# A four-layer graph network on one core: the head and the first period given as one list of 403 steps

## The chip, the cores and the metric

The kernel runs on one core of a Trainium2 chip. A core has five engines that run side by side, each with its own queue of instructions in a fixed order: TensorE (PE, matmuls, with weight loads shown as PEld), VectorE (DVE), ScalarE (ACT), GpSimd (POOL) and SyncE (SP, which here only starts transfers). An instruction starts when the one ahead of it on its engine has gone and the semaphores it waits for have come. The metric is the device time of one execution in microseconds; the time before is the median of three runs.

## The reference

The input x has 128 graphs of 128 nodes with 256 features, adj is one 128x128 matrix for all of them. Four layers follow, each on h = relu(layernorm(x)) and each added to x:

```python
h = jnp.maximum(_layernorm(x, axis=-1), 0.0)
x = x + _L0_gnn_ref(h, adj, adj, ...)   # relu of three messages, each times a sigmoid gate of h
h = jnp.maximum(_layernorm(x, axis=-1), 0.0)
x = x + _L1_gnn_ref(h, adj, Wqkv, Wo)   # causal attention with adj as a bias
h = jnp.maximum(_layernorm(x, axis=-1), 0.0)
x = x + _L2_gnn_ref(h, adj, adj, W1, W2, W3)   # three products with adj*adj mixing the nodes
h = jnp.maximum(_layernorm(x, axis=-1), 0.0)
x = x + _L3_gnn_ref(h, adj, W1, b1, g1, be1, W2, b2, g2, be2)   # two linear layers with batchnorm
```

The batchnorms of the last layer take statistics over all graphs, so a second pass follows the first.

## The kernel before

The 128 graphs go in 32 groups of four. `layer0`, `layer1` (attention and the first product of layer 2), `layer2` and `layer3` are Python generators that emit the instructions of one group and yield at the ends of stages; a yield of `SPLIT` marks a place within a stage. `norm` takes the layernorm statistics on DVE (L367, L371), the power -0.5 on POOL (L224 for half a group, L375 to L378 for a whole one) and gives h on ACT (L392). `turn` (L405) transposes h on PE and evicts it with ACT and DVE; `mixed` (L435) multiplies by an adjacency matrix; `seven` (L498) multiplies two 2x2 block matrices with seven block products instead of eight, for which block sums of both operands are needed: `sums` (L447) makes those of the activations, `seven_of` (L234) those of the weights, both on DVE.

Main loop: in period g (L1000) the list `TURN` interleaves the streams A (layer 0 of group g+2), B and b (layer 1 of group g+1 and the start of g+2), C (layer 2 of g) and D and d (layer 3 of g-1 and the start of g). `in_turn` (L88) ties each new instruction to the one before it on its engine, so that the scheduler, which otherwise chooses the order on an engine, keeps the written one. For g of 1 and more this is done for all five engines (`PINNED`, L957), and period 0 is left to the scheduler.

Ahead of the loop stands the head (L982 to L999): group 0 is taken through layers 0 and 1 in two halves of two graphs (streams a and c for layer 0, b and d for layer 1), beside layer 0 of group 1 (A) and the preparation of the weights (p, `prepare`, L278). The string `FILL` gives the order in whole stages, of which only PE's order is kept (`KEPT`). Group 0 uses plain products instead of `seven`, since the block sums of w1, m_qk and w_vo are made only afterwards. The letter w calls `awake(12)`, which puts twelve transposes of the identity on PE (L110); their result is not read.

Preparation in `prepare`: the transposes of Wqkv (wqkvT, L259) and the products m_qk and w_vo (pqk, pvo, L289), then the mask and the square of adj, then the block sums of w2, m_qk, w_vo, w1 and w3, the transposes and sums of the last layer's weights (bw1T, bw2T), the degree normalisation of adj, and the vectors. Ahead of all this stand the transpose of adj (pa) and of the gate weights (pgw) and the two signed adjacency matrices ain and aout. The loads are queued on SP in the order x of group 0 (two halves), gate biases, Wqkv, Wo, edge biases, x of group 1, W1, W2, x of group 2, W3, gate weights, the last layer's weights and vectors; the three gate weight rows for pgw go by POOL's queue.

Of the kernel before, what the change touches and what calls it, by code (L numbers as in the profile page):

```python
# [8 lines left out]
FP = mybir.dt.float32  # L9
# [6 lines left out]
P = 128  # L16
# [6 lines left out]
def kernel(  # L23
# [209 lines left out]

    def seven_of(b, name, extra=None):  # L234


        b11, b21, b12, b22 = quarters(b)
        if extra is None:
            extra = weights.tile([P, 3, b.shape[1] // 2, b.shape[2] // 2], FP, name=f"{name}_s")
        operands = set_of(b, extra)  # L240
        t4n, t1, t2 = operands[3:6]
        nc.vector.tensor_tensor(t1, b12, b11, ALU.subtract)
        nc.vector.tensor_tensor(t2, b22, t1, ALU.subtract)
        nc.vector.tensor_tensor(t4n, b21, t2, ALU.subtract)
        nc.vector.tensor_tensor(b12, b22, b12, ALU.subtract)
        return operands

# [4 lines left out]
    def turned(dst, src, nr, name):  # L252


        ncol = src.shape[-1] // P
        for c in range(ncol):
            pt = bank([P, nr, P], f"{name}_{c}")
            for r in range(nr):
                nc.tensor.transpose(pt[:, r, :], src[:, r, c * P : (c + 1) * P], ident)  # L259
            nc.scalar.copy(dst[:, c, :].rearrange("p (r q) -> p r q", r=nr), pt)  # L260


    pa = bank([P, P], "pa")
    nc.tensor.transpose(pa, adj_sb, ident)
    nc.vector.tensor_copy(adjT, pa)
    pw = bank([P, DC, 3], "pgw")
    for c in range(DC):
        nc.tensor.transpose(pw[:, c, :], gwr[:, c * P : (c + 1) * P], ident[:3, :3])
    nc.vector.tensor_copy(gwT, pw)
    for dst, src in ((ain, adj_sb), (aout, adjT)):  # L270
        nc.vector.tensor_scalar(pos, src, 0.0, None, ALU.is_gt)
        nc.vector.scalar_tensor_tensor(f, src, 0.0, pos, ALU.min, ALU.add)
        nc.vector.tensor_tensor(dst, f, adj_sb, ALU.mult)

    SETS = {}
    plain = {"qv": 0, "u": 0}

    def prepare():  # L278


        turned(wT, wqkv, DC, "wqkvT")
        for dst, l0, right, name in (
            (m_qk, 0, wT[:, DC : 2 * DC, :], "pqk"),
            (w_vo, 2 * DC, wo, "pvo"),
        ):
            for i in range(DC):
                pw = bank([P, D], f"{name}_{i}")
                for j in range(DC):
                    nc.tensor.matmul(  # L289
                        pw, wT[:, l0 + j, i * P : (i + 1) * P], right[:, j, :],  # L290
                        start=(j == 0), stop=(j == DC - 1),
                    )
                nc.scalar.copy(dst[:, i, :], pw)
        yield

        nc.gpsimd.affine_select(
            out=maskb, in_=adj_sb, compare_op=ALU.is_ge, fill=NEG, base=0,
            pattern=[[-1, P]], channel_multiplier=1,
        )
        nc.vector.tensor_tensor(a2T, adjT, adjT, ALU.mult)  # L300
        yield
        SETS["2"] = seven_of(w2, "w2")
        yield

        assert plain == {"qv": 2, "u": 2}
        SETS["q"], SETS["v"] = seven_of(m_qk, "m_qk"), seven_of(w_vo, "w_vo")
        SETS["1"] = seven_of(w1, "w1")
        yield
        SETS["3"] = seven_of(w3, "w3")
        yield  # L310

        turned(bw1T, bw1, FC, "bw1T")
        turned(bw2t, bw2, DC, "bw2T")
        seven_of(bw2t, "bw2t", bw2s)
        nc.sync.dma_start(BW2S, bw2s)
        nc.sync.dma_start(BW2T, bw2t)
        yield

        nc.vector.tensor_tensor(an, adj_sb, ident, ALU.add)
        nc.vector.tensor_tensor(anT, adjT, ident, ALU.add)  # L320
        nc.vector.tensor_reduce(deg[:, 0:1], anT, AX.X, ALU.add)
        nc.vector.tensor_reduce(deg[:, 1:2], an, AX.X, ALU.add)
        nc.vector.scalar_tensor_tensor(
            dscr, an, 1.0, ident, ALU.mult, ALU.mult, accum_out=deg[:, 2:3]
        )
        nc.vector.tensor_tensor(deg[:, 3:4], deg[:, 0:1], deg[:, 1:2], ALU.add)
        nc.vector.tensor_tensor(deg[:, 3:4], deg[:, 3:4], deg[:, 2:3], ALU.subtract)
        inv_sqrt(dinv, deg[:, 3:4], 0.0)
        nc.vector.tensor_scalar(an, an, dinv, None, ALU.mult)
        ph = bank([P, P], "ph")  # L330
        nc.tensor.transpose(ph, an, ident)
        nc.vector.tensor_scalar(ahT, ph, dinv, None, ALU.mult)
        pv = bank([P, NV], "pv")
        nc.tensor.transpose(pv, vrow, ident[:NV, :NV])
        nc.vector.tensor_copy(vecs, pv)
        yield
        nc.scalar.copy(bw1T_12, bw1T[:, 0, F1 // 2 :])
        SETS["b"] = seven_of(bw1T, "bw1T")

# [65 lines left out]
    def turn(dst, h, bs, name):  # L405

        for c in range(DC):
            pt = bank([P, len(bs), P], f"{name}_{c}")
            for k, b in enumerate(bs):
                nc.tensor.transpose(pt[:, k, :], h[:, b, c * P : (c + 1) * P], ident)  # L410
            evict = nc.vector.tensor_copy if c else nc.scalar.copy
            evict(columns(dst, c, bs), pt.rearrange("p b n -> p (b n)"))

    Q = 32
# [20 lines left out]
    def mixed(dst, src, aT, name, evicts, bs=ALL):  # L435

        for c in range(src.shape[-1] // P):
# [7 lines left out]
            yield SPLIT  # L445

    def sums(engine, a, extra, s3=None):  # L447


        a11, a12, a21, a22 = a  # L450
        s3 = a21 if s3 is None else s3
        s1, s2, s4 = (extra[:, i] for i in range(3))
        engine.tensor_tensor(s1, a21, a22, ALU.add)
# [5 lines left out]
        engine.tensor_tensor(s3, a11, a21, ALU.subtract)  # L459
        return a11, a12, s4, a22, s1, s2, s3  # L460

# [78 lines left out]
    def layer0(g, bs=ALL):  # L540
# [9 lines left out]
        if g < 2:  # L550

            hT = tile_of(g, bs, [P, DC, T], "dT", f"h0T_{g}", 2)
            turn(hT, h, bs, f"ph_{tail}")
            yield
            pl = bank([P, n, 3], f"pl_{tail}")
            for k, b in enumerate(bs):
                for c in range(DC):
                    nc.tensor.matmul(
                        pl[:, k, :], hT[:, c, b * P : (b + 1) * P], gwT[:, c, :],
                        start=(c == 0), stop=(c == DC - 1),  # L560
                    )
            nc.vector.tensor_tensor(gl, pl, gate_bias, ALU.add)
        else:
# [56 lines left out]
        else:  # L620
            pc = bank([P, n, P], f"pc_{tail}")
            for k, b in enumerate(bs):
                nc.tensor.transpose(pc[:, k, :], cmb[:, b, :], ident)
            nc.vector.tensor_copy(cmbT[:, mine, :], pc)
        yield
# [16 lines left out]
    def layer1(g, bs=ALL):  # L642
# [14 lines left out]
        if swapped:  # L657
            cut(hT.rearrange("p c t -> p (c t)"), blocks, DC * G)
        else:
            turn(hT, h, bs, f"pt_{tail}")  # L660
        if n == G:
# [29 lines left out]
        else:  # L691
            for i in halves:
                for j in range(DC):
# [7 lines left out]
                    for rr in range(2):  # L701
                        at = (2 * i + rr) * P
                        for c in range(DC):
# [3 lines left out]
                                start=False, stop=(c == DC - 1), skip_group_check=True,  # L707
                            )
                    evict = nc.vector.tensor_copy if j else nc.scalar.copy
                    evict(qv[:, i, j], pb)  # L710
            plain["qv"] += 1
            yield
# [41 lines left out]
        else:  # L754
            pp = bank([P, n, P], f"pp_{tail}")
            for k in range(n):
                nc.tensor.transpose(pp[:, k, :], p[:, k, :], ident)
            nc.vector.tensor_copy(pT, pp)
        yield
# [41 lines left out]
        else:  # L801
            for b in bs:
                pb = bank([P, H1], f"pu_{g}_{b}")
                for c in range(DC):
                    nc.tensor.matmul(
                        pb, mT[:, c, b * P : (b + 1) * P], w1[:, c, :],
                        start=(c == 0), stop=(c == DC - 1),
                    )
                nc.scalar.activation(u[:, b, :], pb, AF.Relu)
            plain["u"] += 1  # L810
            yield
        uT = tile_of(g, bs, [P, HC1, T], "uT", f"uT_{g}", 1)
        yield from mixed(uT, u, a2T, f"pmu_{tail}", (nc.vector.tensor_copy,), bs)
        if bs[-1] == G - 1:
            ex = w.tile([P, 3, HC1 // 2, T // 2], FP, tag="us", name=f"us_{g}", bufs=1)
            US[g] = yield from sums(nc.vector, quarters_t(uT), ex)
        yield
# [159 lines left out]
    def part(f, g):  # L977
# [3 lines left out]

    KEPT = (mybir.EngineType.PE,)  # L982
    FILL = "aacaaccacapcabpccpbdbdAdbdAdddbAbbAdwbAbAAdpppbdp"
    HALVES = range(G // 2), range(G // 2, G)
    stream = {
        "a": layer0(0, HALVES[0]), "c": layer0(0, HALVES[1]), "p": prepare(),
        "b": layer1(0, HALVES[0]), "d": layer1(0, HALVES[1]), "A": part(layer0, 1),
    }
    for k in FILL:
        at = len(nc.cur_bb.bb.instructions)  # L990
        if k == "w":
            awake(12)
        else:
            step(stream[k])
        in_turn(at, KEPT)
    assert all(next(stream[k], k) == k for k in "acbdA")
    bs, ds = part(layer1, 1), stream["p"]
    for _ in range(BEGUN):
        next(bs)  # L999
    for g in range(NG):  # L1000
        if g + AHEAD < NG:
# [7 lines left out]
        for k in TURN if g < LAST else ():  # L1009
            at = len(nc.cur_bb.bb.instructions)  # L1010
            next(stream[k], None)
            if g:
                in_turn(at, PINNED)
        for k in FINAL if g == LAST else ():
# [247 lines left out]
```

## Time and profile before

| what | value |
|---|---|
| median of the runs | 2534.65 us (2533.94 to 2539.27) |
| profiled execution, its own time | 2536.71 us |
| profiled execution, span | 2534.7 us |
| PE, DVE, ACT, POOL busy in the span | 98%, 78%, 47%, 12% |
| PE matmuls | 14832 |
| first matmul of period 1 (p_1_0_x) | 139.67 us |
| first matmul of period 2 (p_2_0_x) | 208.69 us |

The span runs from the first to the last instruction of the profile. In a table by stretches each row has the stretch, its length, and for PE, PEld, DVE, ACT and POOL the busy time with the number of instructions in brackets; then the granted clock of PE (1.00 is full), the mean busy share of the DMA engines, and what they moved in GB/s. In a list by time each row has start, length, engine, line, operation, the tile written and the tiles read, and in square brackets the idle time of the engine ahead of it and what ended that.

### The profile page before, as it was taken

To read this page: it belongs to the slowest core of one execution; us is meant where nothing else is said; L and a number is where in the kernel's file an instruction comes from. 1 tells how busy PE (TensorE), PEld (TensorE's weight loads), DVE (VectorE), ACT (ScalarE), POOL (GpSimd) and SP (SyncE) were. 2 spreads that over 40 slices of the span, in tenths; PEclk is the share of its full clock that TensorE was granted. 3 is DMA by queue.
4 is the path that set the end of the run, shared out by engine and by line. 5 is a ranking of instruction groups with operands and counts; after the bars stand their busy time and mean duration, and the time that the engine had idled before them with its cause. 6 is when DMAs were issued, how large, how long until landed. Compare 5 with 4: busy or idle time off the path is not lost.

```text
span 2534.7 us, 40786 instructions
## 1 busy us (share of the span) xinstructions
PE 2483.4 (98%) x14832; PEld 2246.1 (89%) x14832; DVE 1970.5 (78%) x4861; ACT 1180.4 (47%) x2486; POOL 311.4 (12%) x563
## 2 busy tenths in 40 slices
PE   6999999999999999999999999999999999999996
PEld 5899999999999999999999999999999999888875
DVE  6777787777778877788777777887778777558876
ACT  3444444444444444444444444444444444337766
POOL 1111111111101111111111111111111111000001
PEclk9999999999999999999999999999999999999998
DMA  4112222222221122222222222122222112135559
GB/s 136 32 51 67 67 63 63 59 67 67 59 59 49 54 66 67 67 67 60 59 66 67 59 59 57 51 61 67 68 67 62 59 55 59 34 131 200 174 192 389
DMA packets 115180, 206.54 MB, mean 81 GB/s; under 512 B 11538, under 2 KB 77092, under 8 KB 111012
## 3 DMA queue, kind: packets, MB, share of 16 engines
q1 hardware_dynamic: 108404, 180.80, 23.4%
q0 software_dynamic: 6432, 23.07, 2.6%
q8 instruction: 117, 1.92, 0.3%
q14 instruction: 83, 0.68, 0.1%
q10 hardware_dynamic: 144, 0.07, 0.0%
HBM read 105.20 MB, written 98.70 MB: 80 GB/s over the span
## 4 chain that ended last, share of the span: by engine, by line
PE 94%; DMA 2%; DVE 2%; ACT 1%; POOL 0%; issue 0%; SPq 0%; DVEq 0%; POOLq 0%; ACTq 0%
PE p_x L490 17%; PE p_x L473 9%; PE p_z L490 9%; PE pmu L440 5%; PE p_z L473 4%; PE p_y L490 4%; PE po_x L1134 4%; PE pz_x L490 4%; PE pu_x L473 4%; PE p_y L473 2%; PE pg L440 2%; PE py L764 2%; PE ps L720 2%; PE pm L630 2%; PE pm L440 2%; PE pr L873 2%
## 5 line engine op out<-in xcount | busy, mean ns | idle before, releaser
L392 ACT ACTIVATE h<-x,sh,rs 128x256 f32<-128x256 f32 x512 | 266.7, 590 | 482.9 <-POOL sh L378 471.3
L490 PE MATMUL p_x<-uT,w 128*128 128x256 f32 x1024 | 242.1, 379 | 0.0
L844 ACT ACTIVATE h2T<-h2T 128x512 f32<-128x512 f32 x192 | 121.0, 630 | 256.7 <-DVE h2T L842 256.7
L490 PEld LDWEIGHTS p_x<-uT,w 128*128 128x128 f32 x1024 | 189.8, 190 | 23.2
L375 POOL TENSOR_SCALAR rs<-mv 128x4 f32<-128x4 f32 x124 | 37.2, 300 | 1378.8 <-DVE mv L371 1365.4
L367 DVE BATCH_NORM_STATS2 st<-x 128x6 f32<-128x256 f32 x512 | 185.9, 414 | 3.3
L567 DVE SCALAR_TENSOR_TENSOR gs<-h,gw 128x256 f32<-128x256 f32 x360 | 152.3, 423 | 43.0 <-ACT h L392 31.5
L440 PEld LDWEIGHTS pmu<-a2T,u 128*128 128x128 f32 x1024 | 124.2, 192 | 29.6 <-issue 21.8
L505 ACT COPY p_t<-p_x 128x512 f32<-128x512 f32 (+1 forms) x192 | 97.4, 507 | 76.2 <-PE p_x L473 69.8
L376 POOL TENSOR_TENSOR rs<-rs,nhalf 128x4 f32<-128x4 f32 x124 | 128.7, 1038 | 9.8
L473 PE MATMUL p_x<-w,h2T 128*128 128x128 f32 x1024 | 124.7, 275 | 0.0
L440 PE MATMUL pmu<-a2T,u 128*128 128x128 f32 x1024 | 124.5, 275 | 0.0
L473 PEld LDWEIGHTS p_x<-w,h2T 128*128 128x128 f32 x1024 | 121.9, 192 | 1.7
L490 PE MATMUL p_x<-us,w_s 128*128 128x256 f32 x512 | 121.1, 379 | 0.0
L490 PE MATMUL p_z<-us,w 128*128 128x256 f32 x512 | 121.1, 379 | 0.0
L490 PE MATMUL p_x<-uT,w_s 128*128 128x256 f32 x512 | 121.1, 379 | 0.0
L490 PE MATMUL p_z<-us,w_s 128*128 128x256 f32 x512 | 121.0, 379 | 0.0
L490 PE MATMUL p_y<-uT,w 128*128 128x256 f32 x512 | 120.9, 379 | 0.0
L842 DVE TENSOR_TENSOR h2T<-p_z,p_t 128x512 f32<-128x512 f32 x64 | 44.0, 687 | 89.4 <-PE p_z L490 89.4
L490 PEld LDWEIGHTS p_x<-uT,w_s 128*128 128x128 f32 x512 | 97.1, 190 | 13.4 <-DVE h2T L842 0.3
L490 PEld LDWEIGHTS p_z<-us,w_s 128*128 128x128 f32 x512 | 97.3, 190 | 13.2
L490 PEld LDWEIGHTS p_y<-uT,w 128*128 128x128 f32 x512 | 97.3, 190 | 13.2
(331 smaller groups left out, 5994.2 us busy)
## 6 DMA issues: line engine op xcount, KB each, us to landing
z<-zo SPq DMA_DIRECT2D x62, 512.0 KB, 5.1
zi<-z SPq DMA_DIRECT2D x31, 1024.0 KB, 4.9
x<-x POOLq DMA_DIRECT2D x32, 512.0 KB, 3.4
x<-in_x_dram SPq DMA_DIRECT2D x31, 512.0 KB, 3.9
hc<-h SPq DMA_DIRECT2D x120, 128.0 KB, 2.4
h<-hc SPq DMA_DIRECT2D x30, 512.0 KB, 4.2
out_dram<-x3i SPq DMA_DIRECT2D x30, 512.0 KB, 11.7
x3i<-x SPq DMA_DIRECT2D x20, 512.0 KB, 6.5
```

What stands on the lines that cost most here:

```text
L367: nc.vector.bn_stats(st[:, k, :], xt[:, b, :])
L376: nc.gpsimd.tensor_tensor(rs, rs, nhalf[:, :n], ALU.pow)
L392: nc.scalar.activation(dst, src, AF.Relu, bias=sh[:, k : k + 1], scale=rs[:, k : k + 1])
L440: nc.tensor.matmul(pm[:, k, :], src[:, b, c * P : (c + 1) * P], aT, start=True, stop=True)
L473: nc.tensor.matmul(pb[:, rr, :], a_r[r][:, c, rr * P : (rr + 1) * P], b_r[r][:, c, :wide], start=(first and rr == 0 and c == 0), stop=(c = ...
L490: nc.tensor.matmul(pb[:, jj, :], b_r[r][:, c, at : at + P], a_r[r][:, c, :], start=(first and jj == 0 and c == 0), stop=(c == nk - 1), ski ...
L505: nc.scalar.copy(t, pb)
L567: nc.vector.scalar_tensor_tensor(gs, h[:, b, :], 1.0, gw[:, i, :], ALU.mult, ALU.mult, accum_out=gl[:, k, i : i + 1],)
L630: nc.tensor.matmul(pm[:, r, :], cmbT[:, b, :], h[:, b, :], start=True, stop=True)
L720: nc.tensor.matmul(ps[:, k, :], qv[:, b // 2, c, 0, (b % 2) * P : (b % 2 + 1) * P], hT[:, c, b * P : (b + 1) * P], start=(c == 0), stop=(c ...
L844: nc.scalar.activation(dst, dst, AF.Relu)
L1134: nc.tensor.matmul(pb, BW2R[r][:, c, :], a_r[r][:, c, :], start=(first and c == 0), stop=(c == FC // 2 - 1), skip_group_check=True,)
```

## The change

- `prepare` is cut into five generators: `gate_weights` (i), `attention_weights` (p), `mixing_weights` (m), `network_weights` (n) and `last_weights` (o). They yield after each instruction or small group; `weight_sums` makes the block sums of one weight in four steps.
- The tiles for the block sums of all weights are allocated at once (`SETS`), ahead of the streams.
- `turn`, `layer0` and `layer1` get more `SPLIT` yields between PE's work and its eviction.
- `FILL`, `awake(12)` and the unpinned period 0 give way to `HEAD`, a string of 403 letters. Each letter takes one step of one stream up to its next yield of either kind, and `in_turn` keeps the order on all five engines. The streams are a, c, b, d as before, e and f (layers 0 and 1 of group 1), A (layer 0 of group 2), B (start of layer 1 of group 2), C (layer 2 of group 0), D (start of layer 3 of group 0), and the five chains of weights. The loop then starts at period 1 with the same `TURN`.

```diff
-    def seven_of(b, name, extra=None):
...
+    SETS = {}
+    for k, b in ("2", w2), ("1", w1), ("3", w3), ("q", m_qk), ("v", w_vo), ("b", bw1T):
+        _, nk, nf = b.shape
+        SETS[k] = set_of(b, weights.tile([P, 3, nk // 2, nf // 2], FP, name=f"set_{k}"))
+
+    def weight_sums(operands):
+
+        b11, b21, b22, t4n, t1, t2, b12 = operands
         nc.vector.tensor_tensor(t1, b12, b11, ALU.subtract)
+        yield
         nc.vector.tensor_tensor(t2, b22, t1, ALU.subtract)
+        yield
         nc.vector.tensor_tensor(t4n, b21, t2, ALU.subtract)
+        yield
         nc.vector.tensor_tensor(b12, b22, b12, ALU.subtract)
-        return operands
+        yield
...
-    def prepare():
-
-
-        turned(wT, wqkv, DC, "wqkvT")
+    def gate_weights():
...
+    def attention_weights():
+
+        yield from turned(wT, wqkv, DC, "wqkvT")
...
+        yield from weight_sums(SETS["q"])
+        yield from weight_sums(SETS["v"])
...
+    def network_weights():
+
+        yield from weight_sums(SETS["2"])
+        yield from weight_sums(SETS["1"])
+        yield from weight_sums(SETS["3"])
+
+    def last_weights():
+
+        yield from turned(bw1T, bw1, FC, "bw1T")
+        yield from turned(bw2t, bw2, DC, "bw2T")
+        yield from weight_sums(set_of(bw2t, bw2s))
+        nc.sync.dma_start(BW2S, bw2s)
+        nc.sync.dma_start(BW2T, bw2t)
+        yield
...
-    KEPT = (mybir.EngineType.PE,)
-    FILL = "aacaaccacapcabpccpbdbdAdbdAdddbAbbAdwbAbAAdpppbdp"
     HALVES = range(G // 2), range(G // 2, G)
+    HEAD = (
+        "iiiaaaapppppcciiipmaapaammapccccacaeeppppppccaccaaceeaacapppppccbbeeecpp"
+        "ecbbbbebdeedAembbbbbededdddbbbeeeodbbmbbeedddbeooommdbooooooobbbbpdddeme"
+        "dbbbeddbedfffoobbbbbbpppdopdbbbbbbbbdCfffffdddfAAffnCCfffffffffAddddfofp"
+        "ofoAddddndpAAfffddddddddfdffddCddfCCCCCCffnnACCCCfCoAACCAACCACCCCCCCCCCA"
+        "AnnnnnAfCCCCCCoffffffAffffCCCCCCACCACCCCfffnCfAAAAABBBffffffffnCConBfBff"
+        "ffoofCCCfCffffooCCfffCCCCCDDDfffffffffffffB"
+    )
+    load_x(AHEAD)
+    ds, bs = layer3(0), layer1(2)
...
-    for k in FILL:
+    for k in HEAD:
         at = len(nc.cur_bb.bb.instructions)
-        if k == "w":
-            awake(12)
-        else:
-            step(stream[k])
-        in_turn(at, KEPT)
...
+        next(stream[k], None)
+        in_turn(at, PINNED)
...
-    for g in range(NG):
+    for g in range(1, NG):
```

## The prediction

> **What bounds the kernel now.** First the page: TensorE (PE) is busy nearly the whole span, and its only thin slice is the first (each slice is 63.4 us).
>
> ```profile
> PE 2483.4 (98%) x14832; PEld 2246.1 (89%) x14832; DVE 1970.5 (78%) x4861; ACT 1180.4 (47%) x2486; POOL 311.4 (12%) x563
> ...
> PE   6999999999999999999999999999999999999996
> ```
>
> Second, the busy times by stretch. From 100 us on PE has no gap: one period of the main loop, 139.67 to 208.69, is 69.02 us of PE busy in 69.02 us. Ahead of 70 us PE is the engine that waits, and in 40 to 60 us its granted clock is 0.84 besides.
>
> ```profile
> 0.00:10.00 10.00, 2.19 (x8) 1.24 (x8) 5.94 (x31) 3.81 (x7) 4.64 (x15) 1.00 0.70 214
> 10.00:20.00 10.00, 6.80 (x25) 5.67 (x26) 5.49 (x22) 3.66 (x11) 0.00 (x0) 1.00 1.05 385
> 20.00:30.00 10.00, 7.91 (x36) 6.46 (x35) 8.58 (x17) 4.19 (x12) 1.62 (x1) 1.00 0.74 209
> 30.00:40.00 10.00, 5.11 (x32) 4.20 (x32) 8.07 (x28) 3.83 (x10) 4.50 (x5) 0.99 0.16 54
> 40.00:50.00 10.00, 8.62 (x50) 7.54 (x50) 4.09 (x11) 3.68 (x12) 0.00 (x0) 0.84 0.00 1
> 50.00:60.00 10.00, 8.80 (x49) 7.30 (x49) 6.80 (x30) 4.92 (x13) 1.39 (x2) 0.83 0.00 0
> ...
> 139.67:208.69 69.02, 69.02 (x424) 62.95 (x423) 54.74 (x138) 31.02 (x67) 9.03 (x18) 1.00 0.22 62
> ```
>
> Third, PE in order of time, for which wait ends last.
>
> ```profile
> 7.88 0.34 PE L268 MATMUL pgw<-ident,wide 3*128 3x3 f32 x2 [4.22 <-DMA wide<-in_L_gnn_loop_gate_dram]
> 8.19 1.40 PE L410 MATMUL ph<-ident,h 128*128 128x128 f32 x4
> ...
> 20.57 2.53 PE L259 MATMUL wqkvT<-ident,wide 128*128 128x128 f32 x12
> ...
> 40.03 2.07 PE L696 MATMUL pqv<-hT,m_qk 128*128 128x256 f32 x4 [4.43 <-ACT hT L412]
> 41.90 1.68 PE L704 MATMUL pqv<-w_vo,hT 128*128 128x128 f32 x8
> 43.42 1.03 PE L696 MATMUL pqv<-hT,m_qk 128*128 128x256 f32 x4
> ...
> 57.07 1.47 PE L110 MATMUL awake<-ident 128*128 128x128 f32 x12
> ```
>
> The 4.43 us stall is the largest after the start: ACT's copy of hT stood behind h of group 1 (38.63), which waited on POOL, which worked beside DVE's two-input weight sums:
>
> ```profile
> 27.58 1.62 POOL L224 TENSOR_TENSOR rs<-rs,nhalf 128x2 f32<-128x2 f32 x1 [18.18 <-DVE rs L222]
> 32.92 0.69 POOL L224 TENSOR_TENSOR rs<-rs,nhalf 128x2 f32<-128x2 f32 x1 [3.72 <-DVE rs L222]
> ...
> 37.08 1.52 POOL L378 TENSOR_TENSOR sh<-sh,rs 128x4 f32<-128x4 f32 x1
> ```
>
> **The measure: lag.** From period 1 on (first matmul p_1_0_x, 139.67 us) PE has the same work in both lists, without a gap before, so the change is worth what it moves that start. I price the work ahead of it at the full-clock pitch of the rows: 128x128 0.1115 us (pmu, 32 in 3.57), 128x256 0.216 (p_x, 8 in 1.73), 128x512 0.431, 128x3 0.115 (pl at 51.40, 16 in 1.85); a transpose is one row, a matmul two. Before: 86x0.1115 + 34x0.115 + 226x0.216 + 300x0.1115 + 20x0.431 + 0.12 = 104.5 us. Lag = 139.67 - 104.5 = 35.2: some 22 idle, the rest half-speed matmuls. The changed list has the same PE work less the 12 transposes of awake: 103.2 us.
>
> **Part by part.** *awake removed*: 12x0.1115 = 1.3 us. *Preparation in five chains, the list over all engines, SPLIT yields*: DVE, ACT, POOL and SP issue exactly the same instructions, only in another order; SP's load queue stands as it was (BW2S and BW2T swap, read only in the second pass). The swap of p through DRAM (pc) now goes whole ahead of that of the gates (cc); there are 19.1 us of PE work from ps to py where there were 13.8, so both stay hidden. So everything else is waits. I walked the new queues: each instruction starts at the later of its engine's last end and its inputs' end plus 0.06 us, with durations from the rows (DVE: 0.33 for 128x256, 0.60 for 128x512, 1.14 for 128x1024, 0.20 for 128x128, bn 0.34; ACT: h 0.50, copies 0.28 and 0.49; pow 0.70, POOL's four-op chain 1.8). PE is at half speed to 24.5 us and again for 3.5 us after group 1's gate (below). The stations:
>
> - *Start.* adj lands at 3.1, adjT and ain now stand ahead of the statistics on DVE (0.83 us), but the second half's no longer do: h of half one ends at 7.75, its transposes start at 7.8 (before 8.19, behind the loop gate's DMA).
> - *wqkv.* Three wqkvT transposes now stand in PE's queue ahead of ph_0_1, so PE waits for that DMA, which before was never waited for. Bounds: in 1-us windows 1.387 MB had moved by 8.0, and wqkv ends the first 1.376 MB; x of group 1 ends 2.43 MB, which had moved by 10.8, and landed at 4.69+7.3 = 12.0. So 8.0 to 9.2; I take 9.0. Each us later costs one.
> - *Layer 0, half one.* DVE's gl of half two waits for pl_2, with half one's gate products queued behind it, and pl_2 waits behind six wqkvT and pqk_0 at half speed. pc_0 at 20.9, 3.7 us later than before (17.18).
> - *Layer 0, half two.* pm_1 at 27.9 (27.48): even. But now group 1's transposes and gate pl_1 are next, 2.7 us of work which before came at 46.96 and 51.40.
> - *Attention.* Half one's first pqv at 32.4 (31.37), half two's at 40.0 (40.03), but bw1T, ps_0 and group 1's gate are behind us, and exp, pc, py follow with PE fed: idle from 32 to 48 is under 1 us in the walk.
> - *Network.* pu_0 at 50.9 (61.15). Work ahead of it is 28.75 us: lag 22.1, as against 61.15 - 28.2 = 32.9 before. From there the walk has no stall up to p_0_0_z at 75.4 (work 53.24, lag 22.1).
> - *Stalls added by hand.* (a) Group 1's h for layer 1: its POOL chain starts beside five two-input weight sums (bw2t, set_q, set_v; 1.6 us). The chain took 2.05 us at 70.78 and 4.0 at 34.63 beside such sums; the walk's 1.8 leaves 0.4 of slack, so the stall is 0 to 1.8; as the sums cover part of the chain, I take 1.0. (b) pm_1_0_0 now follows p_0_z directly, 8.8 us of work after py. Before, h was ready 9.7 us after py began (108.48 to 118.2) and DVE's list adds two oeb products (0.8); four blocks follow ACT's pace: 1.0 us. (c) Drift from pitch rounding, as before between 100 and 139.67: 0.4.
>
> Sum: lag 22.1 + 1.0 + 1.0 + 0.4 = 24.5; p_1_0_x at 103.2 + 24.5 = 127.7 instead of 139.7: **12.0 us saved**. On the profiled execution 2534.7 becomes 2522.7 of span (its own time, 2536.71, 2524.7). The runs' median is 2534.65, 2.06 us under that execution, and 2534.65 - 12.0 = **2522.7 us**.
>
> **Two rules against rows.** Rows first: wqkvT at 20.57 takes 0.21 us per transpose, twice the later 0.111, although PE had been at work off and on since 8.19; the clock record says 1.00 there, so for the start I trust the durations. After the 4.43 us gap it reads 0.50 in 40 to 42, and full speed is back at 43.42, 3.4 us later; in 53.4 to 57, after small gaps and the gate's 128x3 matmuls, it is half again. [...] By the rows, sparse stretches don't warm it and a gate stretch with gaps cools it: 22.1. I take the rows. [...] each 3.5 us at half clock costs 1.6 (73.8 to 75.4 in the walk). [...]
>
> **Rivals.**
> - *The clock stays half from 28 to 50 us.* For: awake is gone, and DVE waits for POOL at each half's norm (0.9 us). Against: the walk's gaps after 32 are each under 0.6. p_0_0_z at 83.4, lag 30.1, plus 2.4 = 32.5; p_1_0_x at 135.7, saving 4.0: 2530.7.
> - *DVE becomes the bound.* In the walk it is busy for 38 of the 47 us from 26 to 73, and its waits are in fixed places now (0.9 at every half's norm, 2.5 at qv of half one); before, from 26 to 139.67, it was busy 81.18 of 113.67 us. If its rows run a tenth longer beside POOL and in-order waits, 4.7 us: saving 7.3, 2527.4. Against: where PE is dense DVE's results are early in the walk.
> - [...]
> - *The gain doesn't arrive*: something outside PE, such as the swap through DRAM of group 2's h, paces period 1. Against: pqv at 145.75 waited for nothing. 2534.6.
> - *Slower: half clock to 75 us.* p_0_0_z at 95.8, lag 42.5 + 2.4, start at 148.1: 2543.1. One more cold us of PE work costs one us; it decides against the change when the half clock lasts past some 58 us.
>
> **How the numbers follow.** Likeliest 0.60 (own range 2519.5 to 2526.5), clock half to 50 us 0.14, DVE bound 0.09, rule right 0.10, no gain 0.04, slower 0.03. The range 2517 to 2530.5 leaves out the last two, most of the second, and the tails. Within 0.2% (5.1 us, about what a measurement of this kernel tells from no change) falls no gain and most of the second case, 0.13; slower 0.03; faster 0.84.
>
> **What would show it.** p_1_0_x near 128 us, and the end as far behind it as before (2395.0 us); pu_0 near 51; wqkvT waiting for its DMA until about 9; DVE's gl waiting for pl near 18; half-speed rows ending by 25 and once more past 32; a POOL chain over 2 us before pt of group 1; a stall of about 1 us at pm of group 1. The prediction is wrong if PE idles over 1 us anywhere between 32 and 75 us, if clock windows below 0.9 last beyond 36 us, or if period 1 is longer than 69.0 us.

## The result, and the profile after

| | before | changed |
|---|---|---|
| median of the runs | 2535.79 us (4 runs) | 2524.94 us (4 runs, 2523.98 to 2525.63) |
| ratio | | 0.9955 [0.9938, 0.9973] |
| profiled execution, span / own time | 2534.7 / 2536.71 us | 2521.3 / 2523.98 us |
| p_1_0_x, first matmul of period 1 | 139.67 us | 125.96 us |
| from there to the end of the span | 2395.03 us | 2395.34 us |

The changed kernel is 10.85 us faster by the medians, where 12.0 were forecast (2522.7, range 2517 to 2530.5). A second set of five runs gave 2524.91 beside 2535.84, ratio 0.9952 [0.9939, 0.9966]. The profiled execution after is the fastest of its four runs and that of before lies above its median, so the two profiles differ by more, 13.4 us of span.

The page of the changed kernel, its engines and the slices (63 us each): PE has 12 instructions less, and the first slice has gone from 6 to 8 tenths.

```profile
PE 2480.3 (98%) x14820; PEld 2243.0 (89%) x14820; DVE 1972.8 (78%) x4861; ACT 1181.2 (47%) x2486; POOL 309.3 (12%) x563
...
PE   8999999999999999999999999999999999999996
```

Its busy times by stretch, with the columns as before (PE, PE's weight loads, DVE, ACT, POOL, clock, DMA):

```profile
10.00:20.00 10.00, 8.26 (x39) 7.11 (x37) 5.97 (x24) 5.50 (x17) 0.00 (x0) 1.00 1.05 385
20.00:30.00 10.00, 9.07 (x45) 7.50 (x45) 8.48 (x28) 5.66 (x14) 2.51 (x5) 0.83 0.65 217
30.00:40.00 10.00, 9.88 (x61) 8.88 (x60) 6.10 (x25) 5.79 (x17) 0.70 (x1) 0.83 0.05 18
40.00:50.00 10.00, 9.97 (x64) 8.23 (x63) 8.98 (x30) 5.11 (x16) 1.25 (x2) 1.00 0.00 1
50.00:60.00 10.00, 10.00 (x52) 7.75 (x52) 9.06 (x32) 5.05 (x10) 2.54 (x5) 1.00 0.01 2
60.00:70.00 10.00, 10.00 (x58) 7.79 (x57) 9.50 (x31) 5.55 (x11) 2.56 (x4) 1.00 0.24 93
70.00:80.00 10.00, 10.00 (x64) 9.21 (x63) 9.80 (x21) 3.93 (x12) 0.00 (x0) 1.00 0.01 2
125.96:194.98 69.02, 69.02 (x425) 62.95 (x423) 54.90 (x137) 31.02 (x67) 7.58 (x16) 1.00 0.20 57
```

PE is full from 40 to 80 us (before: 8.62 and 8.80 of 10 between 40 and 60), and the price is seen in DVE's column: 9.06 to 9.80 of 10 between 50 and 80. Period 1 is the same 69.02 us.

PE of the changed kernel in order of time, the stations of the forecast:

```profile
8.96 1.48 PE L262 MATMUL wqkvT<-ident,wide 128*128 128x128 f32 x6
...
16.63 0.99 PE L584 MATMUL pl<-gwT,h0T 128*128 128x3 f32 x8
18.62 0.30 PE L650 MATMUL pc<-ident,m 128*128 128x128 f32 x1 [0.99 <-DVE m L625]
...
20.59 2.08 PE L658 MATMUL pm<-h,m 128*128 128x256 f32 x4 [1.08 <-DVE m L652]
...
30.92 2.05 PE L724 MATMUL pqv<-hT,m_qk 128*128 128x256 f32 x4
32.77 1.54 PE L732 MATMUL pqv<-w_vo,hT 128*128 128x128 f32 x8
34.15 1.03 PE L724 MATMUL pqv<-hT,m_qk 128*128 128x256 f32 x4
...
49.28 3.70 PE L835 MATMUL pu<-w,mT 128*128 128x512 f32 x8
...
81.79 1.99 PE L516 MATMUL p_x<-uT,set 128*128 128x256 f32 x8 [0.62 <-DVE h2T L874]
...
102.88 1.90 PE L462 MATMUL pm<-a2T,h 128*128 128x128 f32 x8
...
106.35 1.05 PE L462 MATMUL pm<-a2T,h 128*128 128x128 f32 x8
```

No wait in brackets lies between 28.5 and 81 us; the 4.43 us stall of before is gone. The same four rows of pqv take 2.05 us at 30.92 and 1.03 at 34.15: the half clock (granted clock 0.50 from 30.4 to 33.8 us, in windows of half a us). The eight rows at 102.88 take 1.90 where their own pitch gives the 1.05 of 106.35: they follow ACT's h, four rows in 2.07 us from 102.17.

### The profile page after: what moved, and what is told of

It reads as the page before. It is cut to its first block, busy times and chain, and to the rows that moved or that the text cites. A ratio compares the mean times of both kernels' runs of the same rounds, so it can differ in the third digit from the quotient of the medians.

```text
span 2521.3 us, 40758 instructions
## 1 busy us (share of the span) xinstructions
PE 2480.3 (98%) x14820; PEld 2243.0 (89%) x14820; DVE 1972.8 (78%) x4861; ACT 1181.2 (47%) x2486; POOL 309.3 (12%) x563
## 3 DMA queue, kind: packets, MB, share of 16 engines
q8 instruction: 117, 1.92, 0.3%
## 4 chain that ended last, share of the span: by engine, by line
PE 96%; ACT 2%; DVE 1%; issue 0%; DMA 0%; POOL 0%; ACTq 0%; DVEq 0%; POOLq 0%
PE p_x L516 18%; PE p_x L499 9%; PE p_z L516 9%; PE p_z L499 5%; PE pmu L462 5%; PE p_y L516 4%; PE po_x L1174 4%; PE pu_x L499 4%; PE pz_x L516 4%; PE pm L462 2%; PE ps L749 2%; PE p_y L499 2%; PE pg L462 2%; PE pm L658 2%; PE pr L905 2%; PE py L794 2%
## 5 line engine op out<-in xcount | busy, mean ns | idle before, releaser
L516 PEld LDWEIGHTS p_x<-uT,w 128*128 128x128 f32 x1024 | 189.7, 190 | 23.4 <-ACT p_t L531 0.2
L462 PEld LDWEIGHTS pmu<-a2T,u 128*128 128x128 f32 x1024 | 124.2, 192 | 29.2 <-issue 21.5
L516 PE MATMUL p_x<-uT,set 128*128 128x256 f32 x512 | 121.2, 379 | 0.6 <-DVE h2T L874 0.6
L516 PE MATMUL p_x<-us,set 128*128 128x256 f32 x512 | 121.1, 379 | 0.0
L516 PE MATMUL p_z<-us,set 128*128 128x256 f32 x512 | 120.9, 379 | 0.0
L516 PEld LDWEIGHTS p_x<-uT,set 128*128 128x128 f32 x512 | 97.0, 190 | 14.1 <-DVE h2T L874 1.0
L516 PEld LDWEIGHTS p_z<-us,set 128*128 128x128 f32 x512 | 97.2, 190 | 13.2
```

What stands on the lines that cost most here:

```text
L462: nc.tensor.matmul(pm[:, k, :], src[:, b, c * P : (c + 1) * P], aT, start=True, stop=True)
L516: nc.tensor.matmul(pb[:, jj, :], b_r[r][:, c, at : at + P], a_r[r][:, c, :], start=(first and jj == 0 and c == 0), stop=(c == nk - 1), ski ...
```

## The experiments

The measure is again the start of p_1_0_x in each run's trace. It carries the whole effect: from it to the end of the span, all 14 traces (before and after among them) have between 2394.9 and 2396.4 us. Medians come from runs beside the kernel before on the same chip. A trace is one execution, and executions of one kernel spread (the kernel before over 6.1 us in 39 runs, e1 over 7.9 in 12, the changed one over 2.5 in 5), so small differences of p_1_0_x are read with the medians beside them.

| run | p_1_0_x, us | median, us (runs) | ratio to before |
|---|---|---|---|
| before | 139.67 | 2535.79 (4) | |
| before, order kept by all engines (e2) | 162.26 | 2559.12 (4) | 1.0095 [1.008, 1.011] |
| before without awake (e3) | 139.23 | 2536.39 (12) | 1.0002 [0.9994, 1.0011] |
| list on PE alone (e1) | 137.40 | 2532.75 (12) | 0.999 [0.9981, 0.9998] |
| list on PE and ACT (e7) | 130.34 | 2528.21 (1) | |
| list on PE and DVE (e8) | 128.96 | 2526.25 (1) | |
| changed, sums whole (e5) | 133.94 | 2531.91 (20) | 0.9984 [0.9977, 0.999] |
| changed | 125.96 | 2524.94 (4) | 0.9955 [0.9938, 0.9973] |
| changed, again (e11) | 126.98 | 2524.91 (5) | 0.9952 [0.9939, 0.9966] |
| gate behind pqv (e6) | 125.90 | 2523.05 (1) | |
| warm in two waits (e4) | 125.01 | 2523.15 (4) | 0.9951 [0.9934, 0.9967] |
| two waits moved (e9) | 124.56 | 2525.67 (5) | 0.9954 [0.9942, 0.9967] |
| two waits moved, warm (e10) | 124.91 | 2523.44 (5) | 0.995 [0.9938, 0.9963] |
| warm from the start (e12) | 122.05 | 2521.84 (5) | 0.9946 [0.9932, 0.9959] |

The forecast walked the whole list and did not say which part of the change carries the gain. Ahead of the runs my theory was that PE's order carries it; the rivals were the keeping by all engines, the clock (awake), and the small steps.

**Which engines keep the list: e1, e7, e8.**

```diff
     for k in HEAD:
         at = len(nc.cur_bb.bb.instructions)
         next(stream[k], None)
-        in_turn(at, PINNED)
+        in_turn(at, (mybir.EngineType.PE,))   # e7: PE, Activation; e8: PE, DVE
```

e1: 

> The changed kernel with the list of 403 steps kept by PE alone; DVE, ACT, POOL and SP take the scheduler's order in the head. My theory (PE's order, with independent work put into its waits, is the gain): most of it stays, p_1_0_x at 127 to 132 us (125.96 in the changed kernel, 139.67 before). DVE's freed order puts three of w2's sums and the degree sums ahead of the gates, some 1 to 5 us of delay at most. Rival 1 (what gains is that all engines keep a list): the gain is lost, p_1_0_x at 136 or later.

137.40: in this trace 2.3 of the 13.7 us are left. Its execution (2535.43 us) is 2.7 us slower than the median of the twelve; by the medians 3.4 of 10.9 us are left (2536.18 to 2532.75, interval 0.5 to 4.8). My theory, 132 at most, fell either way. PE has the changed kernel's order to the instruction, and waits for engines that have not. The largest loss in the trace of e1 is a chain over three engines. DVE's sums in order of time, then POOL's chain for group 1's h, ACT, and PE:

```profile
57.73 1.22 DVE L246 TENSOR_TENSOR set<-w,set 128x1024 f32<-128x1024 f32 x1
58.87 1.22 DVE L248 TENSOR_TENSOR w<-w 128x1024 f32<-128x1024 f32 x1
```

```profile
56.83 3.36 POOL L395 TENSOR_SCALAR rs<-mv 128x4 f32<-128x4 f32 x1 [5.09 <-DVE mv L391]
60.26 0.23 POOL L397 TENSOR_SCALAR sh<-mv 128x4 f32<-128x4 f32 x1
```

```profile
61.80 1.58 ACT L412 ACTIVATE h<-x,sh,rs 128x256 f32<-128x256 f32 x3 [2.90 <-POOL sh L398]
63.28 0.57 ACT L840 ACTIVATE u<-pu 128x512 f32<-128x512 f32 x1
```

```profile
63.91 2.63 PE L462 MATMUL pmu<-a2T,u 128*128 128x128 f32 x14 [2.84 <-ACT u L840]
66.34 2.79 PE L516 MATMUL p_x<-uT,w 128*128 128x256 f32 x8
```

Six two-input sums stand one behind the other on DVE from 56.55 to 60.09 (the last two are shown), and POOL's first small instruction, 0.26 us in the changed kernel, lasts from 56.83 to 60.19. That the sums held it up is argued from the times alone. ACT has h of group 1 ahead of u, so u waits for that chain; PE waits 2.84 us for u and then runs its next rows partly at half clock (p_x 2.79 us instead of 1.89). A second loss lies earlier, where DVE's order has the statistics of group 1's x ahead of gwT and so waits 3.62 us for that transfer (12.28), and PE's first gate product with it (14.03, not 11.58).

e7: 

> The list kept by PE and ACT alone (p_1_0_x: all five 125.96, PE alone 137.40). If the head-of-queue order on ACT made the loss with PE alone (u of half one behind the h of group 1 that waited for POOL, 2.84 us of PE waiting and a half clock after it), about half comes back: p_1_0_x at 128 to 133. If DVE's free order (sums ahead of gates) made it, 134 or later.

130.34.

e8: 

> The list kept by PE and DVE alone. If ACT's order made the loss with PE alone, p_1_0_x stays at 132 or later. If DVE's order made it, most comes back: p_1_0_x at 126 to 129.

128.96. In e7 the sentence that blames ACT came true, in e8 the one that blames DVE, so the two runs do not share the loss out: of the 11.4 us between the traces of e1 and the changed kernel, ACT's order brings back 7.1 and DVE's 8.4, together more than there is. Where one of them keeps the list, the chain above doesn't form: in e8 the order that ACT gets from the scheduler has u ahead of h again. What is shown is that PE's order alone brings little (2.3 us in the trace, 3.4 by the medians) and one more engine most of the rest. The last 3.0 to 4.4 us are not shared out: in both runs three engines are still free (DVE or ACT, and POOL and SP), and each is one execution. In e8, PE's waits for ACT's pqv_t, 1.39 us ahead of 65.36 and 0.32 ahead of 66.82, are part of them.

**The old order, kept by all: e2.** FILL and the first period of TURN are kept by five engines; the weight sums still come whole, where the program writes them.

```diff
-    KEPT = (mybir.EngineType.PE,)
+    KEPT = PINNED
...
-            if g:
-                in_turn(at, PINNED)
+            in_turn(at, PINNED)
```

> The kernel before with its own two orders (49 letters, and the first period) kept by all five engines. My theory: PE's order still leaves the waits, and sums now go in whole pieces where they are written, so no gain or a loss: p_1_0_x at 138 to 148 us. Rival 1 (what gains is that all engines keep a list): p_1_0_x at 132 or earlier, at least half of the 13.7 us.

162.26: 22.6 us later, beyond my 148. The first 49 letters lose 8.3 (pu_0 at 69.44, before 61.15), the first period 14.3. Its longest wait:

```profile
93.69 0.45 PE L331 MATMUL ph<-ident,wide 128*128 128x128 f32 x1 [10.07 <-DVE wide L329]
```

PE's queue has this transpose of the weight preparation next, and the row of DVE that it waits for stands on DVE behind the sums of w1, w3 and bw2t, the copies uT and the sums us (79.7 to 91.1 us). Keeping an order on all engines is worth nothing by itself: it takes an order that was made for all of them.

**awake removed: e3.**

```diff
-    FILL = "aacaaccacapcabpccpbdbdAdbdAdddbAbbAdwbAbAAdpppbdp"
+    FILL = "aacaaccacapcabpccpbdbdAdbdAdddbAbbAdbAbAAdpppbdp"
```

> The kernel before without its 12 awake transposes. My theory: they are 1.3 us of PE work, 1.5 at the half speed they ran at, in a stretch where PE also waits; p_1_0_x at 138.0 to 139.7 us. Rival 2 (awake or the clock makes up the gain): 135 or earlier if awake was in the way; 141 or later if it kept the clock up, since each 3.4 us more at half clock costs 1.7.

139.23, and the median is the same within 0.1%. The 12 transposes are neither in the way nor of use; rival 2 falls.

**The small steps: e5.**

```diff
     def weight_sums(operands):
         nc.vector.tensor_tensor(t1, b12, b11, ALU.subtract)
-        yield
         nc.vector.tensor_tensor(t2, b22, t1, ALU.subtract)
-        yield
         nc.vector.tensor_tensor(t4n, b21, t2, ALU.subtract)
-        yield
         nc.vector.tensor_tensor(b12, b22, b12, ALU.subtract)
-        yield
+        for _ in range(4):
+            yield
```

> The changed kernel with the four sums of a weight in one step each (at the place of the first of the four), not spread. My theory: a little is lost, since DVE then holds 1.3 (w_vo, m_qk) to 3.6 us (w1, bw1T) in one piece ahead of the evictions behind it: p_1_0_x at 126.0 to 128.5 us. Rival 3 (the small steps are the gain): 131 or later.

133.94: 8.0 us of the 13.7 are lost, past the bound that I set for rival 3; by the medians 6.6 of 10.9. Some 1.0 of the 8.0 is the arrival of wqkv in this run (wqkvT at 9.94 after a wait of 1.02, not 8.96). The granted clock is half for 3.4 us longer than in the changed kernel (21.1 to 24.5 and 31.4 to 38.2), by my estimate up to 1.7 us; whether the sums or chance brought that is open. From pu_0 on, which neither can touch, it is 81.53 us to p_1_0_x against 76.68: 4.9 us. The four sums of w2 on DVE in e5, and PE behind them:

```profile
64.88 1.22 DVE L242 TENSOR_TENSOR set<-w 128x1024 f32<-128x1024 f32 x1
66.14 1.23 DVE L243 TENSOR_TENSOR set<-w,set 128x1024 f32<-128x1024 f32 x1
67.40 1.22 DVE L244 TENSOR_TENSOR set<-w,set 128x1024 f32<-128x1024 f32 x1
68.54 1.22 DVE L245 TENSOR_TENSOR w<-w 128x1024 f32<-128x1024 f32 x1
69.68 0.41 DVE L479 TENSOR_TENSOR hs<-hs,hT 128x256 f32<-128x256 f32 x1
```

```profile
70.24 0.67 PE L697 MATMUL pqv_x<-hs,set_q 128*128 128x256 f32 x2 [2.47 <-DVE hs L479]
```

Four sums of 1.2 us in one piece stand ahead of a block sum of 0.4 us that PE needs; spread one by one, they cost no wait of PE there. My bound was too low because I had put the longest piece at 3.6 us; these four hold DVE for 4.88.

**The half clock: e4, e6.** In the profiled execution of the changed kernel PE's rows are at half speed until 16.6 us, and by the granted clock again from 20.1 to 23.5 and from 30.4 to 33.8 us.

e4 (letter w: eight awake transposes):

```diff
-  ...caccaaceeaac...
+  ...caccwaaceewaac...
     for k in HEAD:
-        next(stream[k], None)
+        if k == "w":
+            awake(8)
+        else:
+            next(stream[k], None)
```

> The changed kernel with eight awake transposes (0.9 us at full speed) in each of two of its waits: before pc_0 (PE waited 17.62 to 18.62) and before pm_0 (19.5 to 20.59). If the half clock of 20.6 to 23.4 us follows from the thin stretch ahead of it, that stretch runs at full speed: pm_0 at 20.6 takes 1.03 us and not 2.08, pqk of 22.88 1.03 and not 1.36, and p_1_0_x comes at 124.4 to 125.2 (125.96 without). If thin work is not what brings the half clock, the 16 transposes only add: p_1_0_x at 125.9 to 127.5.

125.01, as forecast, but by another way. In this execution PE was still at half speed in the first wait, so the 16 transposes took 1.95 and 1.91 us and delayed pm_0 to 22.11. From there on no row is at half speed any more:

```profile
18.23 1.95 PE L110 MATMUL awake<-ident 128*128 128x128 f32 x8
...
22.11 1.10 PE L658 MATMUL pm<-h,m 128*128 128x256 f32 x4
...
31.34 1.11 PE L724 MATMUL pqv<-hT,m_qk 128*128 128x256 f32 x4
```

e6 (steps 81, 82 and 85 of group 1's gate moved behind half one's pqv):

```diff
-  ...deedAembbbbbeded...
+  ...ddAmbbbeeebbeded...
```

> The changed kernel with group 1's gate product (sixteen rows 128x3) and its exp put behind half one's two pqv products. If the 128x3 rows let the clock fall (30.92 to 34.15 us at half speed), pqv starts at 29.5 when hT is copied, runs at 0.216 us per 128x256 row, and p_1_0_x comes at 124.2 to 125.2. If the half clock comes for another reason, pqv keeps a half-speed stretch of about 3.4 us and p_1_0_x stays at 125.8 to 127.

The second half-speed stretch is gone, and the time is not less:

```profile
29.78 1.13 PE L724 MATMUL pqv<-hT,m_qk 128*128 128x256 f32 x4 [0.47 <-ACT hT L433]
...
36.76 0.94 PE L749 MATMUL ps<-hT,qv 128*128 128x128 f32 x6 [0.81 <-DVE qv L739]
```

The pqv rows run at full speed, but DVE's copy of qv now stands behind the gate's later steps, and PE waits for it. What full speed saved went into the two waits shown and a start 0.4 us later (pm_0 at 20.98). That 128x3 rows by themselves let the clock fall is not shown: e4 has them where the changed kernel has them and stays at full speed.

**The changed kernel again: e11.**

> The changed kernel again, to set its median beside that of the two others on the same chip and to see how far the start of the head wanders from run to run: by the arrival of adj and wqkv, and by where the clock rises, p_1_0_x at 125.5 to 126.8. If the gain of the profiled execution (13.4 us of span) is the rule, the ratio to the kernel before is 0.9947 to 0.9953; if that of the first medians (10.85 us), 0.9955 to 0.9960.

Same kernel, another course of the clock: no row is at full speed before 25.6 us, and the later stretch lies from 32.5 to 35.9.

```profile
21.61 2.07 PE L658 MATMUL pm<-h,m 128*128 128x256 f32 x4 [0.93 <-DVE m L652]
...
25.61 1.91 PE L297 MATMUL pvo<-wide,wide 128*128 128x256 f32 x8
...
32.78 1.92 PE L732 MATMUL pqv<-w_vo,hT 128*128 128x128 f32 x8
```

p_1_0_x comes 1.0 us later for it, 0.2 past my range. That is why a single execution can't judge 1 us here, and the stretch from pu_0 to p_1_0_x, 76.68 and 76.67 us in the two executions, can. The ratio of this set, 0.9952, falls into the first of the two ranges, that of the first set, 0.9955, into the second; the spread of the runs doesn't tell them apart.

**The two late waits: e9, e10.** pm_1_0_0 (and its copy mT) goes behind group 2's two pm products, and pv behind the p_x product that waited 0.62 us; e10 has five awake transposes in each of e4's two places besides.

```diff
-  ...CCCCfCoAACCAACC...ACCACCCCfffnCfAAAAABBB...
+  ...CCCCfCAACoCAACC...ACCACCCCffnCAAAfAfABBB...
```

> The changed kernel with two places of the list changed: pm_1_0_0 (with its mT copy) behind the two pm products of group 2, and pv behind the p_x product that waited 0.62 us. If pm_1_0_0 was paced by ACT's h (1.90 us for eight matmuls whose own pitch gives 1.05), 0.85 us go; if the 0.62 us at p_x came from the bank that pv takes, they go too, and if from h2T itself they stay. p_1_0_x at 124.4 to 125.3, against 125.9 in the changed kernel. If both waits are only put off to the next instruction (mT is now copied 1.2 us later, p_x's partner waits in its turn), p_1_0_x stays at 125.7 to 126.5.

> The same two changes and five awake transposes in each of the two waits ahead of pc_0 and pm_0 (five and not eight: at half speed they fill 1.05 us, the length of the wait). If the clock follows from thin work, the half-speed stretches behind 22 us are gone as with eight: 0.9 to 2.2 us less than without them, p_1_0_x at 122.5 to 124.2. If five are too few to hold the clock, they only fill the waits: p_1_0_x as without them, within 0.3 us.

p_1_0_x of e9 falls into the first sentence's range, and for the wrong reason: its rows were at full speed by 16 us (eight of pl in 0.95 at 16.04) and at half speed in one later stretch only, from pm_0 at 19.95 (2.08) to about 25.9. By the medians e9 gains nothing (2525.67, the changed kernel 2524.91 on the same chip). e10 at 124.91 lies in neither of its ranges: from 23 us on no row is at half speed any more, but until 21.5 all are, and its first h came 0.4 us later than in e9. From pu_0 on e9 needs 76.65 us, e10 76.66, the changed kernel 76.68. The two moves bring nothing, the waits are put off:

```profile
80.42 1.99 PE L516 MATMUL p_x<-uT,set 128*128 128x256 f32 x8 [0.78 <-DVE h2T L874]
...
102.34 1.96 PE L658 MATMUL pm<-h,m 128*128 128x256 f32 x8 [0.40 <-DVE m L452]
104.14 1.95 PE L462 MATMUL pm<-a2T,h 128*128 128x128 f32 x16
```

p_x starts as long behind pu_0 as ever (32.51 us in both), so its wait is h2T's own and pv had been hidden in it. The pm rows of group 1 now run at their own pitch (16 in 1.95), but group 2's pm, which took their place, waits for DVE's transpose of m, and DVE has no gap from 95.7 to 103 us. Behind ACT, DVE is the next to be waited for.

**Warm from the start: e12.** 18 awake transposes behind pa, in the 4 us in which PE waits for the first h, and eight in each of e4's places.

```diff
-  iiiaaaapppppcc...
+  iWiiaaaapppppcc...
+        if k in "Ww":
+            awake(18 if k == "W" else 8)
```

> The changed kernel with 18 awake transposes right behind pa, in the 4.0 us in which PE waits for the first h (18 at 0.21 us are 3.8 us), and eight in each of the waits ahead of pc_0 and pm_0. If PE is at half speed until it has been kept at work for some time, full speed begins at 8 to 12 us and not at 16.6 to 22, the rows of 8 to 17 us take half as long (8.4 us of PE work in the changed kernel) as far as wqkv's arrival and the gates' chain on DVE and ACT allow, and p_1_0_x comes at 120.5 to 123.5; the median 2519 to 2522. If the head's first 20 us are set by that chain and not by PE's speed, or the clock rises no earlier, p_1_0_x at 124.5 to 126 and the median 2523 to 2525, as with the eight transposes in the two waits alone.

Both numbers fall into the first sentence: 122.05 and 2521.84 us (2519.71 to 2524.29).

```profile
3.68 3.59 PE L110 MATMUL awake<-ident 128*128 128x128 f32 x18
...
8.55 0.88 PE L262 MATMUL wqkvT<-ident,wide 128*128 128x128 f32 x6
...
12.14 1.03 PE L297 MATMUL pqk<-wide 128*128 128x256 f32 x4
...
28.21 1.92 PE L732 MATMUL pqv<-w_vo,hT 128*128 128x128 f32 x8
```

wqkvT takes 0.88 us (1.48 in the changed kernel), pqk 1.03 (1.91), and pm_0 starts at 16.91, not 20.59. The relapse at the gate is still there (28.21: 1.92 us for eight rows). This is the fastest of all versions: beside the kernel before on the same chip it is 14.4 us faster by the medians (2536.25 to 2521.84), where the changed kernel is 10.9. The intervals of the two ratios overlap; that the gain is real rests on the rows above and on p_1_0_x, 3.9 and 4.9 us ahead of the two traces of the changed kernel.

## Why the prediction was right, point by point

- *The measure.* Right in all 14 traces within 1.5 us: the start of p_1_0_x decides. The rival "the gain doesn't arrive" falls with it.
- *Start; h of half one at 7.75.* ph at 8.20. The forecast put adj at 3.1; in the trace after, pa starts at 3.80, which gave back the 0.4 us. In e11 adj came at 3.37 and ph at 7.77.
- *wqkvT waits for its DMA until 9.0.* It starts at 8.96 in the profiled execution and at 9.22 behind a wait of 0.48 us in e11; 8.55 to 9.94 over the runs of this order. The sizing held.
- *pc_0 at 20.9.* 18.62: the clock came up at 16.6. In e11, where it came later, 19.65. The step was right that gl waits for pl (DVE's gl at 17.66 after 1.34 us for pl) and 1.3 to 2.3 us too dear.
- *Half speed to 24.5 us and 3.5 us after the gate.* e11 has nearly this course, 25.6 and then 32.5 to 35.9: 29.0 us at half speed where 28.0 were forecast. The profiled execution has full speed at 16.6, then 20.1 to 23.5 and 30.4 to 33.8 at half: 23.4 us. So the amount was right in one execution and 4.6 us too long in the other, and the place is not fixed: it differs from execution to execution of one kernel.
- *pu_0 at 50.9.* 49.28, and 50.31 in e11. *p_0_0_z at 75.4, lag 22.1*: 73.94, lag 20.7; e11 74.96, lag 21.7.
- *Stall (a), 1.0 us at pt of group 1.* Nothing: the POOL chain began at 53.20 and took the 2.05 us that were given as a reason, and h was in time nevertheless:

```profile
53.20 0.26 POOL L395 TENSOR_SCALAR rs<-mv 128x4 f32<-128x4 f32 x1 [6.34 <-DVE mv L391]
...
55.05 0.20 POOL L398 TENSOR_TENSOR sh<-sh,rs 128x4 f32<-128x4 f32 x1
```

  The term was over-sized by 1.0. In e1, where other sums fall beside it, the same chain takes 4.9 us: the danger was real, and the list puts the chain where it does no harm.
- *Stall (b), 1.0 us at pm_1_0_0.* 0.85 (1.90 for 1.05). But e9 shows that it is not to be had by a move: DVE holds the next rows at the same pace.
- *Not in the sum:* 0.62 us at 81.79, DVE's h2T. The forecast had said that where PE is dense DVE's results are early. From p_0_0_z to p_1_0_x 2.06 us were added in place of 2.4, so the missing term and the over-sized one nearly cancel, which is luck.
- *Removed awake costs nothing.* Right for the place where it stood (e3: 0.44 us earlier, the medians alike). The forecast did not see that such transposes are worth something elsewhere: 1 us (e4) and 4 us (e12) at p_1_0_x.
- *DVE becomes the bound.* Not in the time, but nearer than its 9% said: from 26 to 73 us DVE is busy for 39.70 us where the walk had 38, for 9.80 of the 10 us before 80, and e5 and e9 fail on it. The price of this rival was loose: a tenth of 38 us is 3.8, not the 4.7 that were subtracted.
- *Clock half to 50 us, and the slower rival:* neither came: the clock is 1.00 from 33.8 us on (35.9 in e11).
- *The rows on the clock.* The forecast gave the changed list what the rows of before showed: half speed at the start, and one more such stretch behind group 1's gate (in the trace of before the granted clock is 0.50 from 39.8 to 43.2 us, behind the 4.43 us gap, and from 53.4 to 56.9). For the dense list as it stands that was right in kind: half speed until 16.6 us, though PE was busy without a gap from 9.9 us on, and in e11 until 25.6. The place is not fixed, though: with 18 transposes in 3.59 us from 3.68 on, full speed is there by 8.55 (e12). The case at 0.10, full speed early and lasting, rested on nothing that the trace of before shows; e12 comes near it in part, with p_1_0_x at 122.05. How much work raises the clock no run shows, nor what lets it fall. In e4 PE is busy for 4.00 of the 4 us from 16 to 20 and again from 20 to 24, and the clock is 1.00 in all windows from 10 to 70 us; in e12 it is busy for 3.74 and 3.41 of them, and the clock is 0.50 from 28 to 30. In the changed kernel PE was busy between 16 and 20 us for more than half of the time and never waited over 1.1 us, and the clock of the next four is 0.57.

```profile
16.00:20.00 4.00, 2.26 (x12) 1.64 (x11) 2.56 (x10) 2.21 (x8) 0.00 (x0) 1.00 1.06 354
20.00:24.00 4.00, 3.42 (x10) 2.81 (x11) 3.35 (x13) 0.95 (x3) 1.55 (x4) 0.57 0.79 245
```

- *The sum.* Lag 24.5 forecast, 22.8 in the profiled execution and 23.8 in e11. Saved 13.7 and 12.7 at p_1_0_x; the medians say 10.9. The forecast's base, one execution of before at 2536.71, was set against the median of three runs, while its p_1_0_x of 139.67 lies in an execution 0.9 us over the later median; that is 0.9 of it, and in e11 the part behind p_1_0_x was 1.1 us longer than in the first execution. Neither is a step of the change. So the mechanism was right, and that 12.0 comes as close to 10.9 is in part luck: at p_1_0_x it was 1.7 and 0.7 us too low, by the medians 1.15 too high.

Open: what decides where the clock falls within the head. The granted clock shows how long each half-speed stretch lasts: 3.4 us twice in the profiled execution and twice in that of before, once in e11, e12 and e6, 3.4 and 6.8 in e5; in e9 rows take twice their time from pm_0 at 19.95 to about 25.9. In the profiled execution the two falls, at 20.1 and 30.4 us, are three times 3.4 us apart, in that of before, at 39.8 and 53.4, four times. Why the lengths and distances are these is not shown, nor how much work keeps the clock up.

## What to carry to other kernels

An order for one engine is worth little when the others fill their queues by their own rule: with PE's queue given alone 2.3 of 13.7 us were left (3.4 of 10.9 by the medians), and an order kept by all that was not made for all cost 22.6. Cut work that nobody waits for (sums of weights) into the smallest steps before placing it: four sums of 1.2 us in one piece cost PE a wait of 2.5 us that the spread ones do not. Where the engine that bounds must wait at the start anyway, give it idle matmuls (here 3.9 us at p_1_0_x), and find one instruction behind which nothing changes, to measure by.

## What was not expected of the hardware

- A small POOL instruction (128x4) lasted 3.36 us in e1 and ended 0.1 us behind the last of six two-input sums on DVE. The longest of these sums takes 1.22. In the changed kernel the same instruction took 0.26 us among six shorter sums (52.94 to 54.51). What makes the difference is open, and the profile's page calls spans on POOL rough.
- Until its first fall, at 20.1 us and in e11 at 32.5, the granted clock of the record is 1.00 in every window, also where rows take twice their time (pqk at 14.92 in the changed kernel: 1.91 us, in e12 1.03). The duration of a known row is the safer sign there.
- The two profiled executions of the changed kernel differ by 2.1 us of span: 1.0 us lies ahead of pu_0, by when the clock rises and when adj and wqkv arrive (wqkvT at 8.96 and 9.22, over the runs of this order 8.55 to 9.94), and 1.1 us behind p_1_0_x.
